# A four-layer graph network on one core: layer 0 multiplied in bfloat16 and float16 parts, and attention's scores in batches of three and five

## The chip, the core and the metric

The kernel runs on one core of a Trainium2 chip, as one program. The metric is the device time of one execution in microseconds (us). The engines that matter are TensorE (PE; its weight loads are listed apart as PEld), VectorE (DVE), ScalarE (ACT), GpSimd (POOL) and SyncE (SP), whose queue issues nearly all DMAs. The engines run side by side, each through its own instructions in their order; semaphores make one wait for another.

## What is computed

There are 3327 nodes with 128 features each (x, float32), and one adjacency matrix adj, 3327 x 3327, float32, whose entries are 0 or 1 (0.48% are 1). Four layers follow one another; each takes h = relu(layernorm(x)) and adds its result to x:

```python
# layer 0                       # layer 1: attention over all nodes; 128 heads (d) of width 8 (h)
x1 = swish((adj @ h) @ W + b)   q, k, v = (x @ W.T).reshape(d, n, 8)  for Wq, Wk, Wv
x2 = swish((adj @ x1) @ W + b)  a = softmax(q @ k.T * d**-0.5 + adj + adj)
                                out = (a @ v).reshape(n, 8 * d) @ Wo.T
# layer 2: a GRU cell on adj @ h       # layer 3: (S + adj) normalised by degree, times h, where S
                                       # keeps the 4 most similar nodes of each row
```

Layer 1 is by far the largest: 128 heads, each with 3327 x 3327 scores, every one of which goes through an exponential.

## The kernel before

**Tiles.** The nodes are cut into T = 26 tiles of 128; node n sits at partition n // 26, tile n % 26. adj is read through its transpose (`adjT`): one tile is 128 rows of 3327 columns, 1.7 MB.

**Layer 0** (lines 275 to 326). Two products with adj, `adj_matmul` (line 194), one after the other. Each loops over the 26 tiles: load the tile into one of three buffers `a`, then seven matmuls of up to 512 columns in float32 (line 204) into seven PSUM banks. Beside it DVE makes passes over each tile: in the first product the column sums that give the degrees (`colsum`, line 292) and, in every second tile, the maximum over the low 16 bits of the words (`bf16_rest`, line 284), which says whether adj is exact in bfloat16; in the second product the absolute maximum (`a_max`, line 295) and the other half of the low bits. In the second product POOL also makes the doubled bfloat16 copy of the tile's first 476 columns (line 272), which attention uses first. After each product the sum is copied out of PSUM (`evacuate`), multiplied by W in groups of four tiles (line 315) and put through the swish. After the first product 26 small matmuls (`dp`, line 310) turn the column sums into the degrees, and DVE copies them out (line 311). At the end the result x is stored to `x1d` (line 326), for the general path.

**Projections** (lines 422 to 498). For each of the 26 row tiles PE makes q, k and v (1024 columns each), ACT copies them out of PSUM, and SP stores them to DRAM. Between the rows a list `early` is worked off, one entry a row: splitting k and q into two parts (`Parting`), the 20 loads for the first four heads (`load_heads(0, 0)`, 16 for k and q and 4 for v, issued at once), the exponentials of the first mask tiles (`exp_of`), and POOL's copies of the keys (`key_pair`). At the end a chain of small operations (lines 484 to 497) reduces four maxima over all partitions and sets the flag `unsafe`.

**Attention** (lines 505 to 631) is written out by hand in a fixed order on all engines (`manual_schedule`). The outer loop runs over 7 chunks of queries (six of 476, one of 471), then over 32 groups of four heads, then over the 26 key tiles t: 5824 steps. In a step:

- `scores` (line 534): four score matmuls, one a head, on 32 rows of PE each (line 547). They go to four buffers `early` and to the tile `late` (one bank in even steps, two in odd steps). The way of a score is a letter: D, DVE adds the mask out of PSUM (line 552); I, PE adds the mask by a product with an identity (`two_i`; the mask tile is already doubled) into the same bank (line 550); G, POOL multiplies by the exponential of the mask afterwards (line 555). Even steps use DDDI, odd steps DDIG.
- ACT takes the exponential of `late` straight from PSUM, once a step (line 553: 476 elements in even steps, 952 in odd ones), and in odd steps the exponential of the pair's five D scores together (line 557: 2380 elements).
- `weigh` (line 559), four steps later: four products with v (line 564), in float32 as two passes each, into one bank `acc`. At the last tile of a group DVE copies `acc` out (`o4`, line 573), and the next group's first product waits for that.

The order on PE is thus, for every step: four scores, one identity product, the four products with v of the step four before.

**Layers 2 and 3** (`tail`) multiply the bfloat16 copy of adj, stored by then as `adj16`, by two float16 parts of the features (`adj_matmul_parts`, line 216; the matmul is line 230). At the very end a flag decides whether a general path runs (a loop of 0 or 1 turns, line 1001); with these inputs it does not.

Of the kernel before, what the change touches and what calls it, by code (L numbers as in the profile page):

```python
# [21 lines left out]
P = 128  # L22
# [11 lines left out]
ROW_PARTS = ((0, 112, T), (112, P - 1, T), (P - 1, P, T - 1))  # L34
SAFE = 60.0
# [19 lines left out]
def kernel(  # L55
# [40 lines left out]
    nc.vector.memset(xs[96:P, T - 1, :], 0.0)  # L96
    for p0, p1, n in ROW_PARTS:
        nc.sync.dma_start(xs[p0:p1, :n], dram(x_in, p0 * T * D, [[T * D, p1 - p0], [D, n], [1, D]]))
# [34 lines left out]

    CUTS = (0, T // 6, T // 2, T)
# [85 lines left out]
    def adj_matmul_parts(agg, parts, pool, on_tile=None):  # L220

        cs = chunks(N, 512)
        with tc.tile_pool(name="adj_ps", bufs=1, space=PSUM) as ps:
            acc = [ps.tile([P, 512], F32, name=f"agg_ps{c}") for c in range(len(cs))]
            for t in range(T):
                a = pool.tile([P, N], BF16, name="a16")
                nc.sync.dma_start(a, adj16[t])
                for i, part in enumerate(parts):
                    for c, (c0, w) in enumerate(cs):
                        nc.tensor.matmul(  # L230
                            acc[c][:, :w],
                            part[:, t, :],
                            a[:, c0 : c0 + w],
                            start=(t == 0 and i == 0),
                            stop=(t == T - 1 and i == len(parts) - 1),
                        )
                if on_tile is not None:
                    on_tile(t)
            evacuate(agg, acc)
# [19 lines left out]
    x1d = dpool.tile([P, T, D], F32, name="x1d")  # L259
# [14 lines left out]

    with tc.tile_pool(name="l0", bufs=1) as pool:
        h, done = layernorm_relu(pool)
        done(T)
        colsum = pool.tile([P, NP], F32, name="colsum")
        nc.vector.memset(colsum[:, N:NP], 0.0)

        def bf16_rest(t, kp, a):

            words = a.bitcast(U16).rearrange("p (n two) -> p n two", two=2)
            nc.vector.tensor_reduce(low_bits[:kp, t : t + 1], words[:kp, :, 0], AX.X, ALU.max)

        def add_degree(t, kp, a):
            if t % 2 == 0:
                bf16_rest(t, kp, a)
            if t == 0:
                nc.vector.tensor_copy(colsum[:, :N], a)  # L290
            else:
                nc.vector.tensor_add(colsum[:kp, :N], colsum[:kp, :N], a[:kp])

        def abs_max(t, kp, a):
            nc.vector.tensor_reduce(a_max[:kp, t : t + 1], a[:kp], AX.X, ALU.max, apply_absolute_value=True)
            if t % 2:
                bf16_rest(t, kp, a)
            a_first.append(doubled(adj_pools[0], a[:kp, : q_chunks[0][1]], t, q_chunks[0][1]))

        for step, lhs in ((0, h), (1, None)):  # L300
            if step == 1:
                lhs = x1
            agg = new_agg(pool)
            adj_matmul(agg, lhs, add_degree if step == 0 else abs_max)
            x1 = pool.tile([P, T, D], F32, name="x1")
            with tc.tile_pool(name="l0_ps", bufs=3, space=PSUM) as ps:
                if step == 0:
                    dp = ps.tile([P, T], F32, name="dp", bufs=1)
                    for t in range(T):
                        nc.tensor.matmul(dp[:, t : t + 1], slots(colsum)[:, t, :], ones, start=True, stop=True)  # L310
                    nc.vector.tensor_copy(deg, dp)
                for t0, n in quads():
                    mp = ps.tile([P, 4, D], F32, name="mp")
                    for j in range(n):
                        nc.tensor.matmul(mp[:, j, :], slots(agg)[:, t0 + j, :], w0_s, start=True, stop=True)
                    y = x1[:, t0 : t0 + n, :]
                    nc.vector.tensor_add(y, mp[:, :n, :], over_f(b0_s, n))
                    nc.scalar.activation(y, y, AF.Silu)  # L318
                    if step == 1:
                        nc.gpsimd.tensor_add(xs[:, t0 : t0 + n, :], xs[:, t0 : t0 + n, :], y)  # L320
# [5 lines left out]
        nc.gpsimd.dma_start(x1d, xs)  # L326
# [65 lines left out]
    def load_heads(c, g):  # L392
# [7 lines left out]
        for i in range(4):  # L400
# [5 lines left out]
        for i in range(4):  # L406
# [4 lines left out]
            )  # L411
        return k_in, q4, v4, []
# [9 lines left out]
    with tc.tile_pool(name="l1", bufs=1) as pool, tc.tile_pool(name="l1_ps", bufs=3, space=PSUM) as ps:  # L422
# [22 lines left out]
        for g in range(2):  # L445
            part = Parting(g)
            for side in range(2):
                early.append(lambda part=part: (part.load(0), part.load(1)) if part.lo[0] is None else None)
                early.append(lambda part=part, side=side: [part.part(side, i) for i in range(4)] and part.store(side))
        first, e_first = [], []  # L450
        early.append(lambda: first.extend(load_heads(0, 0)))
        ahead_part = Parting(2)
        early.append(lambda: (ahead_part.load(0), ahead_part.load(1)))
        early.append(lambda: e_first.extend(exp_of(a, 0) for a in a_first[1::2]))
        early += [lambda: (key_pair(first), key_pair(first))] * (T // 4)
        if T // 2 % 2:
            early.append(lambda: key_pair(first))
        for r in range(T):
# [13 lines left out]
            s = st.tile([P, NH, EA], F32, name="v_st")  # L472
            nc.gpsimd.memset(s[:, :, E : E + 1], 1.0)
# [7 lines left out]

        mx4 = pool.tile([P, 4], F32, name="mx4")
        for i, m in enumerate((q_max, k_max, a_max, low_bits)):
            nc.vector.tensor_reduce(mx4[:, i : i + 1], m, AX.X, ALU.max)
        all4 = pool.tile([P, 4], F32, name="all4")
        nc.gpsimd.partition_all_reduce(all4, mx4, P, bass_isa.ReduceOp.max)
        bound = pool.tile([P, 1], F32, name="bound")
        nc.vector.tensor_mul(bound, all4[:, 0:1], all4[:, 1:2])  # L490
        nc.vector.tensor_scalar_mul(bound, bound, 1.01 * E / 2)
        nc.vector.tensor_add(bound, bound, all4[:, 2:3])
        fits = pool.tile([P, 2], F32, name="fits")
        nc.vector.tensor_scalar(fits[:, 0:1], bound, SAFE / 2, None, op0=ALU.is_le)
        nc.vector.tensor_scalar(fits[:, 1:2], all4[:, 3:4], 0.0, None, op0=ALU.is_equal)
        nc.vector.tensor_mul(unsafe, fits[:, 0:1], fits[:, 1:2])
        nc.vector.tensor_scalar(unsafe, unsafe, -1.0, 1.0, op0=ALU.mult, op1=ALU.add)
        ctx_st.close()
# [6 lines left out]
    WAYS = ("DDDI", "DDIG")  # L505
    PLACES = ((0, 1, 2, 5), (3, 4, 6, 7))
# [12 lines left out]
    with tc.tile_pool(name="at_in", bufs=1) as a_pool, tc.tile_pool(name="at_p", bufs=3) as p_pool, tc.tile_pool(  # L519
# [16 lines left out]
        def scores(step, heads, a2, e_a, p8):  # L536
# [3 lines left out]
            ways, places = WAYS[t % 2], PLACES[t % 2]  # L540
            n_d = ways.count("D")
            late = ps.tile([P, 4 - n_d, 512], F32, name=f"late{4 - n_d}")
            early = [ps.tile([P, 512], F32, name="early", bufs=4) for _ in range(n_d)]
            for i in (*range(n_d, 4), *range(n_d)):
                r = slice(32 * i, 32 * i + 32)
                sp = early[i] if i < n_d else late[:, i - n_d]
                nc.tensor.matmul(sp[:, :we], pairs[t // 2][r, t % 2, :], q4[r, :we], start=True, stop=ways[i] != "I")  # L547
            for i in range(4):
                if ways[i] == "I":
                    nc.tensor.matmul(late[:, i - n_d, :we], two_i, a2[:, :we], start=False, stop=True)  # L550
            for i in range(n_d):
                nc.vector.tensor_tensor(p8[:, places[i], :we], early[i][:, :we], a2[:, :we], op=ALU.add)  # L552
            nc.scalar.activation(p8[:, places[n_d] : places[3] + 1, :we], late[:, :, :we], AF.Exp)  # L553
            if ways[3] == "G":
                nc.gpsimd.tensor_tensor(p8[:, places[3], :we], p8[:, places[3], :we], e_a[:, :we], op=ALU.mult)  # L555
            if t % 2:
                nc.scalar.activation(p8[:, :5, :we], p8[:, :5, :we], AF.Exp)  # L557
# [20 lines left out]
        with tc.manual_schedule(engines=engines):  # L578
# [7 lines left out]
            for j, step in enumerate(steps):  # L586
# [8 lines left out]
                if t % 2 == 0:  # L595
                    p8 = p_pool.tile([P, 8, QW], F32, name="p8")
                scores(step, heads, a_t[t], e_t[t // 2], p8)
                begun[j] = (step, heads[2], p8)
                if j >= ahead:
                    weigh(*begun.pop(j - ahead))  # L600
# [48 lines left out]
    PART = 4096.0  # L649
# [46 lines left out]
    def tail(general):  # L696


        def adj_product(agg, y, parts, on_tile=None):
            if general:  # L700
                adj_matmul(agg, y, on_tile and (lambda t, kp, a: on_tile(t)), a_pool)
            else:
                adj_matmul_parts(agg, parts, a_pool, on_tile)
# [6 lines left out]
        with ExitStack() as s:  # L710
# [42 lines left out]
            with tc.tile_pool(name="l2_tp", bufs=1, space=PSUM) as tps:  # L753
# [9 lines left out]
                adj_product(agg, h, parts, transpose_quad)  # L763
# [53 lines left out]
            with tc.tile_pool(name="l3_hw", bufs=1, space=PSUM) as tps:  # L817
# [18 lines left out]
                adj_product(agg, y, parts, project_quad)  # L836
                while right:
                    project_quad(1)
            nc.gpsimd.tensor_add(xs, xs, over_f(b2_s, T))
# [161 lines left out]
    with tc.For_i(0, n_once, 1):  # L1001
        with tc.tile_pool(name="ga", bufs=1) as pool:
# [63 lines left out]
        nc.sync.dma_start(xs, x1d)  # L1066
# [43 lines left out]
```

## Time and profile before

| | us |
|---|---|
| three runs: median (lowest to highest) | 11189.97 (11184.46 to 11197.54) |
| the profiled execution, its own time | 11195.14 |
| its span, first to last instruction | 11193.4 |
| PE, ACT, DVE, POOL busy | 10850.5, 10199.3, 9343.1, 6016.3 |
| first matmul of layer 0; of its second product | 26.2; 199.4 |
| first matmul of the projections | 381.2 |
| first addition of attention on DVE; last copy of `acc` | 576.2; 10475.2 |

The profile is one execution. Its page gives the busy time of each engine, the share of 40 slices, the chain that ended last, and the costliest groups of instructions; a group's line shows the source line, the engine, what is written from what, the shape, the count, then the busy time in us, the mean of one in ns, and the idle time ahead of it with what ended it. The trace behind it also gives the busy times of any stretch, the instructions in order of time, and who waited for whom. An instruction's duration reaches from its start to its result; instructions overlap on one engine, so what one costs its engine is the distance from its start to the next start. The granted TensorE clock was 0.989 on average, and 1.00 throughout attention.

### The profile page before, as it was taken

What the parts mean: (1) busy time and instruction counts of PE and PEld (TensorE: products, weight loads), DVE (VectorE), ACT (ScalarE), POOL (GpSimd) and SP (SyncE); (2) the same over time, 40 slices, a digit from 0 to 9 for tenths busy, and PEclk for the clock granted to TensorE, in tenths of its full rate; (3) what the DMA queues carried; (4) which work ended last, traced back from release to release, by engine and by line L of the source; (5) the groups of instructions that cost most, each with busy time, mean ns of one, the idle gap of its engine ahead of it and who ended that gap; (6) DMA issues with size and microseconds to landing.
All of it is one profiled execution on the core that took longest, in us unless ns stands there. A gap on an engine that the chain in (4) does not pass through costs nothing. (4 is left out here: it accounts for less than half of the span.)

```text
span 11193.4 us, 209350 instructions
## 1 busy us (share of the span) xinstructions
PE 10850.5 (97%) x79530; PEld 3005.9 (27%) x79530; DVE 9343.1 (83%) x15429; ACT 10199.3 (91%) x9152; POOL 6016.3 (54%) x6964
## 2 busy tenths in 40 slices
PE   9899999999999999999999999999999999999996
PEld 4322222222222222222222222222222222222453
DVE  8588888888888888888888888888888888888656
ACT  0399999999999999999999999999999999999522
POOL 0277777555555555555555555555555555555203
PEclk9899999999999999999999999999999999999998
DMA  7755554333333333333333333333333332333432
GB/s 264 238 129 120 123 127 109 65 64 64 68 64 62 67 66 63 68 65 61 68 66 63 66 66 61 67 66 61 66 66 61 66 63 55 61 58 58 135 113 97
DMA packets 417541, 942.25 MB, mean 84 GB/s; under 512 B 67936, under 2 KB 345937, under 8 KB 380940
## 3 DMA queue, kind: packets, MB, share of 16 engines
q1 hardware_dynamic: 412762, 918.98, 37.4%
q8 instruction: 627, 10.27, 0.4%
q0 software_dynamic: 3760, 9.78, 0.3%
q14 instruction: 392, 3.21, 0.1%
HBM read 788.78 MB, written 139.71 MB: 83 GB/s over the span
## 5 line engine op out<-in xcount | busy, mean ns | idle before, releaser
L552 DVE TENSOR_TENSOR p<-early,a 128x476 f32<-128x476 f32 (+1 forms) x14560 | 8426.4, 646 | 1369.4 <-PE early L547 1297.5
L557 ACT ACTIVATE p<-p 128x2380 f32<-128x2380 f32 (+1 forms) x2912 | 7568.4, 2599 | 0.4
L564 PE MATMUL acc<-p,v 128*9 128x476 f32 (+1 forms) x46592 | 5748.5, 564 | 15.3 <-ACT p L557 1.4
L553 ACT ACTIVATE p<-late 128x476 f32<-128x476 f32 (+1 forms) x5824 | 5315.4, 1175 | 13.8 <-DMA q<-qt 10.2
L555 POOL TENSOR_TENSOR p<-p,e 128x476 f32<-128x476 f32 (+1 forms) x2912 | 3528.1, 1212 | 3204.3 <-ACT p L553 2998.6
L547 PE MATMUL late<-q,k 32*128 32x476 f32 (+1 forms) x8736 | 2798.2, 478 | 99.5 <-ACT p L553 39.7
L547 PE MATMUL early<-q,k 32*128 32x476 f32 (+1 forms) x14560 | 2843.6, 478 | 9.4 <-DVE p L552 9.4
L419 POOL CAST k<-k_in 128x256 fp32r<-128x256 f32 x2912 | 1936.5, 697 | 886.4 <-DMA k_in<-kt 339.4
L547 PEld LDWEIGHTS late<-q,k 32*128 32x128 f32 x8736 | 1065.4, 181 | 4890.4 <-ACT p L553 4186.2
L550 PE MATMUL late<-a,two_i 128*128 128x476 bf16 (+1 forms) x5824 | 2180.8, 374 | 0.0
L547 PEld LDWEIGHTS early<-q,k 32*128 32x128 f32 x14560 | 1113.0, 181 | 9.9 <-DVE p L552 9.9
L564 PEld LDWEIGHTS acc<-p,v 128*9 128x9 f32 x46592 | 695.2, 88 | 1272.6 <-issue 1185.8
L550 PEld LDWEIGHTS <-two_i 128*128 128x128 bf16 x5824 | 556.2, 96 | 1329.0 <-issue 1329.0
L189 ACT COPY agg<-agg_ps 128x512 f32<-128x512 f32 x15 | 8.2, 591 | 485.5 <-PE agg_ps L204 290.6
L230 PE MATMUL agg_ps<-a,part 128*128 128x512 bf16 (+1 forms) x1092 | 227.0, 369 | 4.3 <-ACT agg L928 3.2
L272 POOL TENSOR_SCALAR a<-a_in 128x476 bf16<-128x476 f32 (+2 forms) x156 | 221.1, 1417 | 0.5
L272 POOL TENSOR_SCALAR a<-a 128x476 bf16<-128x476 f32 (+1 forms) x26 | 36.4, 1400 | 288.1 <-DMA a<-in_adjT_dram 288.1
L923 PE MATMUL sp<-yT,hT 128*128 128x512 f32 (+1 forms) x364 | 170.7, 610 | 12.3 <-ACT agg L928 6.4
L204 PE MATMUL agg_ps<-a,h 128*128 128x512 f32 (+2 forms) x364 | 148.2, 570 | 26.2 <-DVE h L164 26.2
L573 DVE COPY o<-acc 105x476 f32<-105x476 f32 (+1 forms) x224 | 144.5, 645 | 4.6 <-PE acc L564 4.6
L204 PE MATMUL agg_ps<-a,x 128*128 128x512 f32 (+2 forms) x364 | 145.3, 562 | 0.6 <-ACT x L318 0.6
L230 PEld LDWEIGHTS <-part 128*128 128x128 f16 x1092 | 108.6, 99 | 117.7 <-issue 10.3
(236 smaller groups left out, 2592.0 us busy)
## 6 DMA issues: line engine op xcount, KB each, us to landing
k_in<-kt SPq DMA_DIRECT2D x1792, 207.9 KB
v<-vd SPq DMA_DIRECT2D x896, 117.0 KB
a<-in_adjT_dram SPq DMA_DIRECT2D x50, 1663.5 KB
a<-adj SPq DMA_DIRECT2D x78, 831.8 KB
q<-qt SPq DMA_DIRECT2D x1536, 29.8 KB
a_in<-in_adjT_dram SPq DMA_DIRECT2D x125, 238.0 KB
adj<-a SPq DMA_DIRECT2D x156, 119.0 KB
vd<-v_st SPq DMA_DIRECT2D x25, 576.0 KB
```

The lines of the kernel that those rows point to most:

```text
L204: nc.tensor.matmul(acc[c][:, :w], lhs[:kp, t, :], a[:kp, c0 : c0 + w], start=(t == 0), stop=(t == T - 1))
L230: nc.tensor.matmul(acc[c][:, :w], part[:, t, :], a[:, c0 : c0 + w], start=(t == 0 and i == 0), stop=(t == T - 1 and i == len(parts) - 1),)
L272: nc.gpsimd.tensor_scalar(a2[:kp, :w], a, 2.0, None, op0=ALU.mult)
L419: nc.gpsimd.tensor_copy(k, slots(k_in)[:, t : t + 2, :])
L547: nc.tensor.matmul(sp[:, :we], pairs[t // 2][r, t % 2, :], q4[r, :we], start=True, stop=ways[i] != "I")
L550: nc.tensor.matmul(late[:, i - n_d, :we], two_i, a2[:, :we], start=False, stop=True)
L552: nc.vector.tensor_tensor(p8[:, places[i], :we], early[i][:, :we], a2[:, :we], op=ALU.add)
L553: nc.scalar.activation(p8[:, places[n_d] : places[3] + 1, :we], late[:, :, :we], AF.Exp)
L555: nc.gpsimd.tensor_tensor(p8[:, places[3], :we], p8[:, places[3], :we], e_a[:, :we], op=ALU.mult)
L557: nc.scalar.activation(p8[:, :5, :we], p8[:, :5, :we], AF.Exp)
L564: nc.tensor.matmul(acc[32 * i : 32 * i + EA, :w], v4[:kp, i, t, :], p8[:kp, PLACES[t % 2][i], :w], start=(t == 0), stop=(t == T - 1),)
L923: nc.tensor.matmul(sp[:, c0 : c0 + w], slots(zT)[:, t, :], z2T[:, cols], start=True, stop=False)
```

## The change

Four things are changed, all in one diff.

**Layer 0.** Each tile of adj is doubled and copied to bfloat16 by ACT as it comes (`a16`, two buffers), and PE multiplies that copy: in the first product by two float16 parts of h (scaled by 4096), in the second by three bfloat16 parts of x1. DVE's pass over each tile is either the column sum or the low bits; the absolute maxima leave. `colsum` is spread over both products, so `dp` stands after the second one. The float32 version stays as `layer_0_general`, in the general path, together with `projections_general`; the store to `x1d` goes.

**x and the projections.** x is loaded in three pieces. The 20 loads of the first heads go out in pieces between the rows; `v_st` is four fixed tiles whose ones are set once.

**The scores.** A pair of steps is made together: three scores (heads 1, 2, 3 of the even step, all D), then the products with v of an earlier step, then five scores (head 0 of the even step and all heads of the odd one) and two identity products. `late` has three banks and is read by one exponential of 1428 elements.

**The flags.** `a_max` is taken in the products of layers 2 and 3 from the bfloat16 copy, in every second tile of each; the chain that sets `unsafe` moves behind the second of them.

The core of the diff:

```diff
-    for p0, p1, n in ROW_PARTS:
-        nc.sync.dma_start(xs[p0:p1, :n], ...)
+        for t0, t1 in zip(CUTS, CUTS[1:]):
+            for p0, p1, n in ROW_PARTS:
+                ...
+                    nc.sync.dma_start(xs[p0:p1, t0 : t0 + m], ...)
...
+        parts = two_parts(pool)
+        parts3 = [pool.tile([P, T, D], BF16, name=f"part3_{i}") for i in range(3)]
+        with tc.tile_pool(name="adj_in", bufs=3) as a_pool, tc.tile_pool(name="adj_half", bufs=2) as half_pool:
...
+                _, done = layernorm_relu(ln, lambda h, p, n: split(parts, h, p, scale=PART))
...
+                for step, lhs in ((0, parts), (1, parts3)):
...
+                            load_rows(a, adjT, t, 0, N)
+                            a16 = half_pool.tile([P, N], BF16, name="a16")
+                            nc.scalar.activation(a16[:kp], a[:kp], AF.Copy, scale=2.0)
+                            for i, part in enumerate(lhs):
+                                for c, (c0, w) in enumerate(cs):
+                                    nc.tensor.matmul(acc[c][:, :w], part[:kp, t, :], a16[:kp, c0 : c0 + w], ...)
+                            if t % 2 == step:
+                                bf16_rest(t, kp, a)
+                            else:
+                                nc.vector.tensor_add(colsum[:kp, :N], colsum[:kp, :N], a[:kp])
...
+                            if step == 0:
+                                rest = own.tile([P, 4, D], F32, name="x1_rest", bufs=2)
+                                nc.scalar.copy(parts3[0][:, q], y)
+                                nc.vector.tensor_sub(rest[:, :n], y, parts3[0][:, q])
+                                nc.gpsimd.tensor_copy(parts3[1][:, q], rest[:, :n])
+                                nc.vector.tensor_sub(parts3[2][:, q], rest[:, :n], parts3[1][:, q])
...
-        early.append(lambda: first.extend(load_heads(0, 0)))
+        pieces, e_first = [], []
+        first = load_heads(0, 0, pieces)
+        early += pieces[:4]
...
-    WAYS = ("DDDI", "DDIG")
-    PLACES = ((0, 1, 2, 5), (3, 4, 6, 7))
+    WAYS = ("IDDD", "DDIG")
+    PLACES = ((5, 0, 1, 2), (3, 4, 6, 7))
+    BATCHES = (((0, 1), (0, 2), (0, 3)), ((0, 0), (1, 2), (1, 3), (1, 1), (1, 0)))
...
+            late = ps.tile([P, 3, 512], F32, name="late")
+            for n, batch in enumerate(BATCHES):
+                if n == 1:
+                    between()
+                for odd, i in batch:
+                    way, place = WAYS[odd][i], PLACES[odd][i]
+                    sp = ps.tile([P, 512], F32, name="early", bufs=4) if way == "D" else late[:, place - 5]
+                    r = slice(32 * i, 32 * i + 32)
+                    nc.tensor.matmul(sp[:, :we], pairs[t // 2][r, odd, :], q4[r, :we], start=True, stop=way != "I")
+                    if way == "D":
+                        nc.vector.tensor_tensor(p8[:, place, :we], sp[:, :we], a2s[odd][:, :we], op=ALU.add)
+            for odd, i in BATCHES[1]:
+                if WAYS[odd][i] == "I":
+                    nc.tensor.matmul(late[:, PLACES[odd][i] - 5, :we], two_i, a2s[odd][:, :we], start=False, stop=True)
+            nc.scalar.activation(p8[:, 5:, :we], late[:, :, :we], AF.Exp)
+            nc.scalar.activation(p8[:, :5, :we], p8[:, :5, :we], AF.Exp)
...
                 if t % 2 == 0:
-                    p8 = p_pool.tile([P, 8, QW], F32, name="p8")
-                scores(step, heads, a_t[t], e_t[t // 2], p8)
+                    p8 = scores(step, heads, a_t[t : t + 2], lambda: weigh(*begun.pop(j - ahead)) if j >= ahead else None)
+                else:
+                    times_e(step, p8, e_t[t // 2])
+                    if j >= ahead:
+                        weigh(*begun.pop(j - ahead))
...
+            def seen(t, a):
+                if t % 2 == half:
+                    nc.vector.tensor_reduce(a_max[:, t : t + 1], a, AX.X, ALU.max, apply_absolute_value=True)
...
     with tc.For_i(0, n_once, 1):
+        layer_0_general()
+        projections_general()
```

## The prediction

> **What bounds the kernel now.** I read the busy time by stage first, since one average over five stages says little.
>
> ```profile
> core 0: us, PE busy (x) PEld busy (x) DVE busy (x) ACT busy (x) POOL busy (x), PEclk, DMA share, GB/s
> 20.00:175.00 155.00, 148.25 (x364) 70.14 (x365) 149.20 (x53) 6.84 (x10) 0.00 (x0) 1.00 0.71 260
> 381.00:576.00 195.00, 152.40 (x320) 64.77 (x320) 65.16 (x62) 80.12 (x80) 33.63 (x71) 0.87 0.88 264
> 576.00:10475.00 9899.00, 9784.52 (x75704) 2407.52 (x75704) 8533.33 (x14783) 9893.06 (x8814) 5812.77 (x6734) 1.00 0.36 71
> ```
>
> Layer 0's products with adj (the first is row 1) are bound by PE, with DVE close behind; the projections (row 2) by DMA; and attention, 88% of the span, by ACT: 9893 of 9899 us busy. PE has 9785 there, so it is a near second. Attention is 2912 pairs of key tiles, so a pair takes 9899 / 2912 = 3.399 us. The groups by form give what PE and ACT do in a pair, and the timeline when it starts:
>
> ```profile
> L557 ACT ACTIVATE p<-p 128x2380 f32<-128x2380 f32 x2496 | 6491.5, 2601 | 0.4
> L564 PE MATMUL acc<-p,v 128*9 128x476 f32 x38400 | 4744.6, 565 | 11.9 <-DVE o L573 0.7 <-POOL p L555 0.2
> L547 PE MATMUL early<-q,k 32*128 32x476 f32 x12480 | 2439.1, 478 | 9.4 <-DVE p L552 9.4
> L564 PE MATMUL acc<-p,v 128*9 128x471 f32 x6400 | 783.5, 560 | 3.4 <-ACT p L557 1.4
> L547 PE MATMUL early<-q,k 32*128 32x472 f32 x2080 | 404.5, 476 | 0.0
> ```
>
> ```profile
> 5001.26 2.55 ACT L557 ACTIVATE p<-p 128x2380 f32<-128x2380 f32 x1
> ...
> 5002.76 0.49 PE L547 MATMUL late<-q,k 32*128 32x476 f32 x2
> ...
> 5003.18 0.37 PE L550 MATMUL late<-a,two_i 128*128 128x476 bf16 x1
> 5003.34 1.79 ACT L553 ACTIVATE p<-late 128x476 f32<-128x476 f32 x2
> 5003.48 0.12 PEld L564 LDWEIGHTS acc<-p,v 128*9 128x9 f32 x8 [0.21 <-issue]
> 5003.48 0.99 PE L564 MATMUL acc<-p,v 128*9 128x476 f32 x8
> 5004.39 0.18 PEld L547 LDWEIGHTS late<-q,k 32*128 32x128 f32 x1 [0.80 <-ACT p L553]
> 5004.40 0.48 PE L547 MATMUL late<-q,k 32*128 32x476 f32 x1
> ...
> 5004.63 2.57 ACT L557 ACTIVATE p<-p 128x2380 f32<-128x2380 f32 x1
> ```
>
> ACT's row is read start to start: 2.08 for the long exponential, 1.29 for the two from PSUM, together 3.37; there is no gap in it. PE's row: four scores .42, the identity .30, eight products with v .92, so 1.64 a step and 3.28 a pair. PE waits for ACT by about .1 us in every second step and has no other slack. **Whatever adds .1 us to PE's pair is paid in full.**
>
> **Attention, ACT's side.** L553's two calls a pair become one over 1428 elements. From single starts between 2000 and 9000 us, 476 elements hold ACT .447 and 952 hold it .845: .398 for each 476 and .049 fixed. One call costs 3 x .398 + .049 = 1.243, so ACT's pair falls by .049 to 3.32. If ACT remained the bound, that would be 143 us.
>
> **PE's side.** Per pair the scores now go in batches of four and four; in the change three, then five, with products for v after each. Head 0's 32 rows of PE are in the batch of five twice, so I let its fifth score follow the first instead of running beside it. What does one score stream? Durations grow by 478 - 476 = 2 ns for four columns more, while L564's passes grow by 565 - 560 = 5 ns for five: a score's column costs half of what a column of L564 costs. L564's two passes start .403 apart (.85 ns a column), so 476 score columns stream for .20 us; the rest of the .42 is its own weights (0.18 in the PEld row, which starts with the scores and not ahead of them) and .04 for four at once.
> - Batch of three to L564: not in the trace; between .38 (rows where the last score came alone: .376 from its start to L550) and .42. I take .41.
> - Batch of five: .42 + .20 = .62 if the fifth's weights load while the first streams, up to .42 + .20 + .18 = .80 if not. The nearest row is L564's PEld row above: eight weight loads, the second pass's four in the same columns, are all done within .12 us while the first pass still streams. So I take .62.
> - Two identity products in a row: .30 + .20 = .50 (adj's bfloat16 products at L230 take 2.81 us a tile for 6654 columns, .42 ns each).
> - L564 twice: 1.84.
> Sum .41 + .92 + .62 + .50 + .92 = 3.37, .09 above now and .05 above ACT's new pair. PE becomes the bound.
>
> The Trainium skill ("TensorE: Matmul & The Clock Gate", Part 3, "The mechanism") speaks against this change: a weight load overlaps matmuls in flight only where the row group differs, while Part 2 of the page also admits a load into a background buffer. L564's row, all 128 rows in both passes, sides with Part 2; by Part 3's sentence the sum would be 3.55.
>
> **Group ends.** The accumulator is copied out once in 13 pairs (224 times):
>
> ```profile
> 5050.81 0.99 PE L564 MATMUL acc<-p,v 127*9 127x476 f32 x8
> ...
> 5051.91 0.65 DVE L573 COPY o<-acc 105x476 f32<-105x476 f32 x1
> 5052.60 0.12 PEld L564 LDWEIGHTS acc<-p,v 128*9 128x9 f32 x8 [0.35 <-DVE o L573]
> ```
>
> From the last product to the first of the next group at least 1.80 us pass. Today a whole step (1.64) lies between, so .15 is lost, under ACT's cover. In the change only the batch of three does (.92 + .41 = 1.33): .46 is lost, on the engine that bounds. A group takes 13 x 3.37 + .46 = 44.27, 224 of them 9917; minus 10 for the narrower last chunk; plus 31 for the six groups whose 13 mask exponentials (.49 each on ACT) keep ACT the bound (13 x 3.81 = 49.5). 9938 against 9899: **+39 us**. POOL (5813 busy) and DVE (five additions at .56 are 2.8 a pair) stay covered.
>
> **Layer 0.** Now a tile costs PE 5.58 us (float32, starts of consecutive loads) in both products. In bfloat16 two parts cost 2.81, three 4.21. New on ACT: a copy of 3327 elements, 2.8 us by the slope above, beside idle ACT. DVE keeps one pass of 3.61 a tile (the maxima leave). A tile's load is 1.70 MB; at the best rate of the first 60 us (.85 MB in 2 us) it takes 4.0.
> - First product: by the built program's order DVE still meets the mask's identity from POOL (now at 12.6 us) within the first layernorm piece, and its passes over tiles 0 and 2 stand between pieces, so buffers come free late: by my count tile 6 lands near 56 us, then 4.0 to 4.1 a tile; the last is multiplied by 139 (now 174.5).
> - Between the products the 12 us of dp leave, the split into three parts comes. Second product from about 159, PE-bound at 4.21 x 26 = 110, to 268 (now 344.6).
> - dp comes back after it, and DVE's copy of deg waits for it ahead of the layernorm: 2 + 12 + 12 + 22 = 48 to the first projection, now 36.5. So 316 against 381: **-65 us**. Bounds -95 (no load stalls) and -30 (only the first product's gain).
> - Projections: 26 rows, DMA-bound. The 20 loads of the first heads now stand in one block at 471 to 491 us, while PE is 4.3 of 20 us busy; spread over rows they overlap the stores. -15 (0 to -20).
> - Moved work: the 26 maxima (3.61) go to the two bfloat16 products of layers 2 and 3, where DVE is half idle: 0. The small chain with POOL's all-reduce, mask bounds, goes from the start of attention to the path before layer 3's features: +3. The copy of xs to x1d goes, off the path.
>
> **Sum:** +39 - 65 - 15 + 3 = -38 us on the profiled execution's 11195 (span 11193): 11157. The median of the runs shown is 5 lower, inside their spread; I say **11155**.
>
> **Rivals.**
> 1. The fifth score's weights don't hide: +.18 a pair, 13 x 224 x .18 = +524: 11680, slower. For it: nowhere does the trace put the same 32 rows twice in a row. Against: L564's loads. It decides early: beyond .013 us more on PE's pair (38 / 2912) the whole gain is gone.
> 2. PE's pair is cheaper than my sum (.38 for the three, no .04 for crowding) and ACT bounds: a pair of 3.32 to 3.35 gives 30 to 150 us less: about 11040, at the very best 10920. For it: the solo .376 rows. Against: the loss at group ends.
> 3. Layer 0 gives only the first product's 30 us, the projections nothing (DMA at .88 already): 11195 + 39 - 30 = about 11200, no change.
> That the general path runs after all would double the time; adj is 0 and 1, exact in bfloat16, so I give it nothing.
>
> **Chances.** Forecast, 11100 to 11220: .5. Rival 1, whole or in part: .18. Rival 2: .2. Rival 3: .12. Below 11168 (0.2%, about what a measurement of this kernel tells from no change) lie .3 of the first and all of rival 2, so faster .5; same .14 + .07 = .21; slower .29. The range takes rival 2's likely value and a part of rival 1: 11000 to 11300; it leaves out the whole of rival 1.
>
> **What would show it.** PE busiest in attention, ACT idle by some .05 a pair before its call on late; from the batch of five's first score to the first identity product .62 (.80 says rival 1); L564 waiting for o by about .46 a group; first projection near 316 us. If ACT is still busy without gaps, rival 2 holds. I'm wrong if the first projection starts after 350, or the fifth score starts its stream after its own weights.

## The result, and the profile after

| | before | after |
|---|---|---|
| five runs each: median (lowest to highest), us | 11189.82 (11184.46 to 11197.54) | 11244.57 (11243.61 to 11246.85) |
| ratio, 95% interval | | 1.0049 (1.0034 to 1.0064) |
| span of the profiled execution | 11193.4 | 11241.9 |
| first matmul of the projections | 381.2 | 334.8 |
| first addition of attention; last copy of `acc` | 576.2; 10475.2 | 520.7; 10519.2 |

The change made the kernel slower, by half a per cent, where a gain of a third of a per cent was forecast. The stages say where: layer 0 gave 46 us and the projections 9 (195.0 to 185.9), attention took 100 more (9899.0 to 9998.5) and the tail 4.5 (718.2 to 722.7). -46.4 - 9.1 + 99.5 + 4.5 = +48.5, the difference of the spans.

The busy times by stage after the change (first and second product of layer 0, projections, attention):

```profile
core 0: us, PE busy (x) PEld busy (x) DVE busy (x) ACT busy (x) POOL busy (x), PEclk, DMA share, GB/s
20.00:148.00 128.00, 86.59 (x364) 37.87 (x363) 111.65 (x38) 85.48 (x33) 1.45 (x1) 0.93 0.88 344
171.00:288.00 117.00, 113.26 (x546) 54.07 (x545) 90.43 (x30) 73.16 (x28) 30.89 (x25) 0.97 0.80 306
335.00:521.00 186.00, 149.03 (x319) 62.76 (x319) 64.23 (x54) 79.48 (x78) 25.82 (x46) 0.92 0.90 277
521.00:10519.00 9998.00, 9888.54 (x75705) 2446.75 (x75705) 8550.06 (x14783) 9881.84 (x5902) 5814.23 (x6734) 1.00 0.36 70
```

In attention (last row) ACT has 2900 instructions fewer, and the stage is 116 us longer than ACT's busy time; before, the difference was 6. PE's busy time has grown by 104. That does not yet say that PE bounds: the busy times of the two still lie within 7 us of each other. The chain that ended last decides it, here its two lines from the page, shares of the span by engine and by line:

```profile
PE 86%; ACT 5%; DVE 3%; issue 2%; DMA 2%; POOL 1%; SPq 0%; DVEq 0%; ACTq 0%; POOLq 0%
PE acc L661 45%; PE early L641 15%; PE late L646 12%; PE late L641 10%; ACT p L648 2%; ACT p L647 2%; DVE o L670 1%; PE agg_ps L237 1%; DMA a<-in_adjT_dram 1%; POOL rows L1072 0%; ACT e L398 0%; PE yp L840 0%; DMA qf<-qk_st 0%; DVE colsum L325 0%; PE pp L539 0%
```

The end hangs on PE through nearly all of attention. What PE waits for stands in the page's groups, and one pair in the timeline shows PE's order (L641 are scores, L646 identity products, L661 products with v, L647 and L648 ACT's two exponentials):

```profile
L661 PE MATMUL acc<-p,v 128*9 128x476 f32 (+1 forms) x46592 | 5760.7, 564 | 86.4 <-DVE o L670 86.1
L647 ACT ACTIVATE p<-late 128x1428 f32<-128x1428 f32 (+1 forms) x2912 | 3966.0, 1362 | 124.8 <-PE late L646 118.1
```

```profile
5001.87 2.18 ACT L648 ACTIVATE p<-p 128x2380 f32<-128x2380 f32 x1
...
5002.68 0.48 PE L641 MATMUL late<-q,k 32*128 32x476 f32 x3
5002.69 0.28 PEld L641 LDWEIGHTS early<-q,k 32*128 32x128 f32 x2
5002.69 0.69 PE L641 MATMUL early<-q,k 32*128 32x476 f32 x2
...
5003.31 0.57 PE L646 MATMUL late<-a,two_i 128*128 128x476 bf16 x2
...
5003.81 0.99 PE L661 MATMUL acc<-p,v 128*9 128x476 f32 x8
...
5004.00 1.36 ACT L647 ACTIVATE p<-late 128x1428 f32<-128x1428 f32 x1
...
5004.73 0.48 PE L641 MATMUL early<-q,k 32*128 32x476 f32 x3
...
5005.14 0.99 PE L661 MATMUL acc<-p,v 128*9 128x476 f32 x8
5005.26 2.18 ACT L648 ACTIVATE p<-p 128x2380 f32<-128x2380 f32 x1
```

PE's row has no gap; ACT's long call starts 3.39 after the one before. Medians of the distances between 2000 and 9000 us: three scores to L661 .417, that to the batch of five .917, from there to the identity products .628, these to L661 .506, that to the next three .917: 3.385 in all. The last row of the trace that matters is a group's end:

```profile
5037.61 0.99 PE L661 MATMUL acc<-p,v 127*9 127x476 f32 x8
...
5038.53 0.48 PE L641 MATMUL early<-q,k 32*128 32x476 f32 x3
5038.69 0.65 DVE L670 COPY o<-acc 105x476 f32<-105x476 f32 x1
...
5039.40 0.22 PEld L661 LDWEIGHTS acc<-p,v 128*9 128x9 f32 x8 [0.69 <-DVE o L670]
5039.40 1.08 PE L661 MATMUL acc<-p,v 128*9 128x476 f32 x8 [0.39 <-DVE o L670]
...
5040.41 0.48 PE L641 MATMUL late<-q,k 32*128 32x476 f32 x3
```

L661 follows the three scores after .87 and not .417, and the block that then starts is 1.01 long and not .917. The kernel before does not show this second cost, though there, too, the first products of most groups, with their weight loads, wait for the copy (.13 us in the median, behind identity products):

```profile
5052.61 0.99 PE L564 MATMUL acc<-p,v 128*9 128x476 f32 x8
...
5053.52 0.48 PE L547 MATMUL late<-q,k 32*128 32x476 f32 x2
```

That block is .91 long, so the wait alone does not explain the 1.01; why it is longer behind scores was not tried. A group, from one copy of `acc` to the next, takes 44.53 us (median), before 44.04.

### The profile page after: what moved, and what is told of

Its sections match the earlier page's. It is cut to its first block, busy times and chain, and to the rows that moved or that the text cites. A ratio compares the mean times of both kernels' runs of the same rounds, so it can differ in the third digit from the quotient of the medians.

```text
span 11241.9 us, 207120 instructions
## 1 busy us (share of the span) xinstructions
PE 10873.6 (97%) x79712; PEld 2994.8 (27%) x79712; DVE 9379.7 (83%) x15446; ACT 10347.5 (92%) x6301; POOL 6015.1 (54%) x6948
## 4 chain that ended last, share of the span: by engine, by line
PE 86%; ACT 5%; DVE 3%; issue 2%; DMA 2%; POOL 1%; SPq 0%; DVEq 0%; ACTq 0%; POOLq 0%
PE acc L661 45%; PE early L641 15%; PE late L646 12%; PE late L641 10%; ACT p L648 2%; ACT p L647 2%; DVE o L670 1%; PE agg_ps L237 1%; DMA a<-in_adjT_dram 1%; POOL rows L1072 0%; ACT e L398 0%; PE yp L840 0%; DMA qf<-qk_st 0%; DVE colsum L325 0%; PE pp L539 0%
## 5 line engine op out<-in xcount | busy, mean ns | idle before, releaser
L648 ACT ACTIVATE p<-p 128x2380 f32<-128x2380 f32 (+1 forms) x2912 | 6348.9, 2180 | 0.0
L661 PE MATMUL acc<-p,v 128*9 128x476 f32 (+1 forms) x46592 | 5760.7, 564 | 86.4 <-DVE o L670 86.1
L647 ACT ACTIVATE p<-late 128x1428 f32<-128x1428 f32 (+1 forms) x2912 | 3966.0, 1362 | 124.8 <-PE late L646 118.1
L641 PE MATMUL early<-q,k 32*128 32x476 f32 (+1 forms) x14560 | 3413.7, 457 | 10.8 <-DVE p L643 9.6
L641 PEld LDWEIGHTS early<-q,k 32*128 32x128 f32 x14560 | 1372.3, 182 | 2333.5 <-DVE p L643 2329.0
L646 PE MATMUL late<-a,two_i 128*128 128x476 bf16 (+1 forms) x5824 | 1674.7, 369 | 0.0
L641 PE MATMUL late<-q,k 32*128 32x476 f32 (+1 forms) x8736 | 1415.7, 479 | 22.7 <-ACT p L647 22.5
L661 PEld LDWEIGHTS acc<-p,v 128*9 128x9 f32 x46592 | 715.1, 88 | 1917.9 <-issue 1762.6
L641 PEld LDWEIGHTS late<-q,k 32*128 32x128 f32 x8736 | 547.3, 181 | 2345.9 <-ACT p L647 2172.3
L646 PEld LDWEIGHTS <-two_i 128*128 128x128 bf16 x5824 | 330.7, 97 | 964.8 <-issue 964.8
L314 PE MATMUL agg_ps<-a,part 128*128 128x512 bf16 (+2 forms) x910 | 199.9, 381 | 73.6 <-ACT a L311 65.1
L311 ACT ACTIVATE a<-a 128x3327 bf16<-128x3327 f32 (+1 forms) x52 | 154.9, 2979 | 78.7 <-DMA a<-in_adjT_dram 56.9
```

What stands on the lines that cost most here:

```text
L314: nc.tensor.matmul(acc[c][:, :w], part[:kp, t, :], a16[:kp, c0 : c0 + w], start=(t == 0 and i == 0), stop=(t == T - 1 and i == len(lhs) - 1),)
L641: nc.tensor.matmul(sp[:, :we], pairs[t // 2][r, odd, :], q4[r, :we], start=True, stop=way != "I")
L646: nc.tensor.matmul(late[:, PLACES[odd][i] - 5, :we], two_i, a2s[odd][:, :we], start=False, stop=True)
L647: nc.scalar.activation(p8[:, 5:, :we], late[:, :, :we], AF.Exp)
L661: nc.tensor.matmul(acc[32 * i : 32 * i + EA, :w], v4[:kp, i, t, :], p8[:kp, PLACES[t % 2][i], :w], start=(t == 0), stop=(t == T - 1),)
```

## The experiments

Theory T, from these rows: attention is bound by PE; the fifth score (.20 a pair) and the bare group end (.455 + .1) cost more than ACT's merged call saves. Its rivals: the loss comes from another part of the change (R2), or from the merged call and its single buffer `late`, for which both engines wait (R1). Differences below are against the kernel before in the same set of runs; on that scale the change itself stands at +55 us.

### The old order of scores in the changed kernel, and the new order alone in the old one

```diff
 # the first, on the kernel after
-    WAYS = ("IDDD", "DDIG")
-    PLACES = ((5, 0, 1, 2), (3, 4, 6, 7))
-    BATCHES = (((0, 1), (0, 2), (0, 3)), ((0, 0), (1, 2), (1, 3), (1, 1), (1, 0)))
+    WAYS = ("DDDI", "DDIG")
+    PLACES = ((0, 1, 2, 5), (3, 4, 6, 7))
...
 # and scores() and the order of the step as in the kernel before; the second is the reverse, on the kernel before
```

> The changed kernel with the attention steps of the kernel before (batches of four and four, one call on late a step, each score with its own key tile). Theory T (the attention's new order of scores costs 100 us because it makes PE the bound; layer 0, x and the projections gain 46 + 9, the tail loses 4.5): attention back at 9899, first projection at 335, 11190 - 51 = 11139 us. Rival R2 (the attention is slower because of something else that the change moved, such as the maxima and the chain behind them, the first heads' loads or the buffers' places): attention stays near 9998 and the time near 11240.

> The kernel before with nothing but the new order of scores and the merged call on late. T: attention 9998 instead of 9899, all else as before: 11190 + 100 = 11290 us. R2: near 11190. If this and the run with the old scores add up to the whole change (+100 - 51 = +49), the parts do not act on each other.

Measured: old order in the new kernel 11143.2 us, ratio 0.9959 (0.9945 to 0.9973), -45 us; attention 9893. New order alone 11294.2 us, ratio 1.0094 (1.0077 to 1.011), +106 us; attention 9998. Both as T says, R2 is out, and the parts add up (-45 + 106 = +61 against +55, within what the runs scatter). So the forecast's "faster" would have come true for everything but the scores.

### Four and four

```diff
-    BATCHES = (((0, 1), (0, 2), (0, 3)), ((0, 0), (1, 2), (1, 3), (1, 1), (1, 0)))
+    BATCHES = (((0, 1), (0, 2), (0, 3), (1, 0)), ((0, 0), (1, 2), (1, 3), (1, 1)))
```

> The changed kernel with head 0's second score moved from the batch of five to the batch of three: four and four, with the merged call on late and its key tiles kept. T: PE's pair loses the .20 of the fifth score, 3.385 - .20 = 3.18, so ACT bounds again at 3.32 a pair; with some of the group's end still open a group takes 43.2 to 43.7 instead of 44.53, so 185 to 300 us less than the changed kernel: 10945 to 11060. Rival R1 (it is the merged call and the one buffer of late that both engines wait for, not the fifth score): no change, near 11240.

Measured: 11165.2 us, ratio 0.998 (0.9971 to 0.999), -23 us, so 77 less than the change, not the 185 to 300 of T nor R1's nothing. From a batch of four to the identity products it is .422 (median): the fifth score had cost .628 - .422 = .206. But the group only falls to 44.14. The timeline of that run, first PE (a batch with `late`, then one without), then DVE (its additions), then ACT (L648 is the long call):

```profile
5014.84 0.48 PE L641 MATMUL late<-q,k 32*128 32x476 f32 x3
5014.85 0.48 PE L641 MATMUL early<-q,k 32*128 32x476 f32 x1
5015.26 0.57 PE L646 MATMUL late<-a,two_i 128*128 128x476 bf16 x2
5015.76 0.99 PE L661 MATMUL acc<-p,v 128*9 128x476 f32 x8
5016.68 0.86 PE L641 MATMUL early<-q,k 32*128 32x476 f32 x4
5017.47 0.99 PE L661 MATMUL acc<-p,v 128*9 128x476 f32 x8
```

```profile
5014.11 2.90 DVE L643 TENSOR_TENSOR p<-early,a 128x476 f32<-128x476 f32 x5 [0.67 <-PE early L641]
```

```profile
5010.61 2.19 ACT L648 ACTIVATE p<-p 128x2380 f32<-128x2380 f32 x1
...
5014.03 2.18 ACT L648 ACTIVATE p<-p 128x2380 f32<-128x2380 f32 x1
...
5017.35 2.19 ACT L648 ACTIVATE p<-p 128x2380 f32<-128x2380 f32 x1
```

At 5016.68 four scores last .86: three start together and the fourth .38 later, at 5017.06; the last addition of the pair before had ended at 5014.11 + 2.90 = 5017.01. Between 2000 and 9000 us the fourth score comes late in 961 of 2055 pairs, and each time it starts .055 to .057 us after an addition has ended. ACT's calls are 3.42 and 3.32 apart by turns. Part of the expected gain went into a new wait, and the last run on the scores, below, settles which.

### The group's end: hide it, or take its wait away

```diff
 # the first: the new group's first products with v go behind the batch of five
-                    p8 = scores(..., lambda: weigh(*begun.pop(j - ahead)) if j >= ahead else None)
+                    end = j > ahead and t == ahead
+                    p8 = scores(..., lambda: weigh(*begun.pop(j - ahead)) if j >= ahead and not end else None)
+                    if end:
+                        weigh(*begun.pop(j - ahead))
 # the second: the copy does not read the accumulator
-                nc.vector.tensor_copy(o4[: 96 + EA, :w], acc[: 96 + EA, :w])
+                nc.vector.tensor_copy(o4[: 96 + EA, :w], p8[: 96 + EA, 0, :w])
```

> The changed kernel, but once a group, where the first products with v of a new group would follow the last of the old one with only three scores between them, they are put behind the batch of five and the identity products, so that the copy of the accumulator has 1.55 us of PE's work to hide behind and not .42. T: the .455 that PE waits there and the .1 or so in the next block go: .45 to .55 x 223 groups = 100 to 125 us less, 11120 to 11145. Rival: ACT gets its input no sooner because late is late either way, or other work of the group sets its length: less than 40 us.

> The changed kernel, but the copy at the end of a group reads a row block of p8 in SBUF instead of the accumulator, so the first product with v of a new group need not wait for it (left out: the attention's result does not reach the output; all else runs). T: the .455 that PE waits per group and the .1 behind it go, 223 x .45 to .55 = 100 to 125 us less: 11120 to 11145, a group 43.98 to 44.08 instead of 44.53. Rival: ScalarE or another wait takes the place, since ScalarE has only .06 of slack a pair (13 x .06 = .8 a group): less than 60 us.

The second came out as T said: 11124.5 us, ratio 0.994 (0.9923 to 0.9957), so 123 less than the change; a group takes 43.98, .544 less than 44.53, and 223 x .544 = 121. 43.98 / 13 = 3.383 is PE's pair once more.

The first went the other way: 11275.2 us, ratio 1.0076 (1.006 to 1.0093), +87 us, so 33 slower than the change. Its PE at a group's end:

```profile
5009.36 0.99 PE L661 MATMUL acc<-p,v 127*9 127x476 f32 x8
5010.28 0.48 PE L641 MATMUL early<-q,k 32*128 32x476 f32 x3
5010.97 0.49 PE L641 MATMUL late<-q,k 32*128 32x476 f32 x3 [0.20 <-ACT p L647]
5010.98 0.48 PE L641 MATMUL early<-q,k 32*128 32x476 f32 x1
5011.71 0.48 PE L641 MATMUL early<-q,k 32*128 32x476 f32 x1 [0.25 <-DVE p L643]
5012.12 0.57 PE L646 MATMUL late<-a,two_i 128*128 128x476 bf16 x2
5012.63 1.78 PE L661 MATMUL acc<-p,v 128*9 128x476 f32 x16
```

The wait for the copy is gone, but the eight scores now take 1.85 in place of .417 + .628. The batch of five comes .92 earlier, when ACT has not yet emptied `late` (0.20), and its last score needs the bank of the first, whose addition stands on DVE behind the copy of `acc` (0.25). A group grows to 44.65. The step was moved past the queue that frees its buffers, which I had not counted.

### Four and four with the shared bank free

```diff
 # on the kernel with batches of four and four
-                        nc.vector.tensor_tensor(p8[:, place, :we], sp[:, :we], a2s[odd][:, :we], op=ALU.add)
+                        s_in = a2s[odd] if (odd, i) == (1, 1) else sp
+                        nc.vector.tensor_tensor(p8[:, place, :we], s_in[:, :we], a2s[odd][:, :we], op=ALU.add)
```

> The run with batches of four and four came to 11165, where T had said 10945 to 11060: its long exponentials start 3.32 and 3.41 apart by turns, and in every second pair the fourth early score starts .38 after the third. Ring theory: the fifth score that VectorE adds to in a pair shares a bank with the fourth of the next pair, whose product must wait until VectorE's last addition has read it. Here that one addition takes adj's tile twice and does not read the score (left out: one of eight heads' scores), so the bank is free at once; VectorE's work stays. Ring theory: pairs 3.32 throughout and .4 at the group's end, a group 43.55 to 43.65 instead of 44.14, about 115 us less, 11040 to 11055. Rival (VectorE's work itself, or the group's end, sets it): 11150 or more.

Measured: 11067.4 us, ratio 0.9892 (0.9875 to 0.9908), 98 less than four and four (115 expected); the median group is 43.62. ACT in that run:

```profile
5004.65 1.43 ACT L648 ACTIVATE p<-late 128x1428 f32<-128x1428 f32 x1
5005.89 2.26 ACT L649 ACTIVATE p<-p 128x2380 f32<-128x2380 f32 x1
5007.97 1.43 ACT L648 ACTIVATE p<-late 128x1428 f32<-128x1428 f32 x1
5009.21 2.27 ACT L649 ACTIVATE p<-p 128x2380 f32<-128x2380 f32 x1
```

Nearly four of five pairs take 3.31 to 3.34, as here 1.24 + 2.08 = 3.32: the forecast's figure for ACT, to the hundredth. VectorE's additions are not shorter than in the run without the edit (the changed one takes .646 us in the median, the others .644), so it is the bank and not VectorE's work; and the merged call with its one buffer `late` is still there, so R1 is out. So the ring is shown: five additions a pair go through four banks; with a batch of four early scores all four banks must be empty at once, that is after DVE's last addition of the pair before, and DVE starts its additions only when the scores are there. A batch of three leaves a bank over; that is what three and five buys, and the fifth score is its price.

### Layer 0: VectorE's passes, x in pieces, buffers

```diff
 # 1: no pass over the low bits
-                            if t % 2 == step:
-                                bf16_rest(t, kp, a)
-                            else:
+                            if t % 2 != step:
 # 2: x whole
-        for t0, t1 in zip(CUTS, CUTS[1:]): ...
+        for p0, p1, n in ROW_PARTS:
+            nc.sync.dma_start(xs[p0:p1, :n], dram(x_in, p0 * T * D, [[T * D, p1 - p0], [D, n], [1, D]]))
 # 3: with the old scores, three operations of the start on POOL
-                nc.vector.memset(colsum, 0.0)            # and the copy of ident to two_i, and last_row
+                nc.gpsimd.memset(colsum, 0.0)
 # 4: one more buffer for adj's tiles
-        with tc.tile_pool(name="adj_in", bufs=3) as a_pool, ...
+        with tc.tile_pool(name="adj_in", bufs=4) as a_pool, ...
```

> The changed kernel without the pass of VectorE over every second tile that collects adj's low bits (left out: the test whether adj is exact in bfloat16). Theory L (layer 0 gains 46 and not 65 because VectorE, which works off its queue in order, holds the first tiles' buffers until 61 us and puts two tile passes of 3.61 between the third-part splits): the loads reach their pace of 4.2 a tile some 8 us earlier, the first product ends at 140 instead of 148, the second starts 3 to 7 us closer behind it, first projection at 320 to 324 instead of 335, total 11230 to 11234. Rival (the loads alone set the start, and the gap between the products is PE's and ScalarE's): first projection at 332 or later.

> The changed kernel with x loaded whole, as before, instead of in three pieces of columns. In the changed kernel VectorE begins the first layernorm piece at 3.9 us, before it waits for TensorE's identity matrix (from POOL at 10.4); whole, x lands later and that piece's 2.3 us move behind the wait. If the pieces help: first matmul 2 to 4 us later than 24.6, first projection 337 to 340, total 11247 to 11250. If VectorE's queue or the loads of adj hide it: first projection at 335, no change.

> The kernel with the old order of scores (layer 0, x and projections as changed), with three things taken from VectorE's queue at the start and given to POOL: the bfloat16 identity (VectorE waits for it until 10.7), the last-row mask (until 11.7) and the memset of colsum (2.83). Theory L: VectorE is through its first tiles some 6 us earlier, first product ends at 142 instead of 148, total 6 us below the run with the old scores' 11143: 11137. Rival (the loads alone set the start): 11143.

> The changed kernel with four buffers for layer 0's tiles of adj instead of three. Theory B (what the forecast missed in layer 0 is the loads' own: the DMA engines stand idle at 22 to 30, 36 to 38 and 43 to 46 us because no buffer is free, and the last tile of the second product, which loads slowly, is asked for too late): the first product ends some 12 us earlier (136 instead of 148 to 153), the second product's last two tiles no longer wait (111 to 113 us instead of 116 to 117), first projection at 316 to 322, total 11226 to 11232. Rival (VectorE's and ScalarE's passes over the tiles set the pace at the start): first product still takes 124 us from its first matmul, first projection at 332 to 338, no change.

Six profiles with the same layer 0 (the change, old scores, four and four with and without the free bank, both runs on the group's end) put the scale: first matmul at 24.6 to 27.4, first product 123 to 126 long (first to last matmul, mean 124.9), second 113.3 to 117.3 (mean 115.0), first projection at 332 to 338, in the mean 335.3. In the table the stages are those of one profile each; the times of kernels 1 and 2 cannot be told from the change's. Kernel 4 stands at +47 us against the change's +55, and kernel 3 at -50 against -45 for the old scores alone; both intervals overlap with those that they are compared with.

| kernel | first matmul | first product | second product | first projection | time, ratio and interval |
|---|---|---|---|---|---|
| 1 no low bits | 24.8 | 121.2 | 113.7 | 330.8 | 11240.6, 1.0042 (1.0025 to 1.0059) |
| 2 x whole | 31.2 | 126.8 | 113.9 | 342.1 | 11249.4, 1.005 (1.0033 to 1.0067) |
| 3 start on POOL, old scores | 20.6 | 124.0 | 115.7 | 330.2 | 11142.0, 0.9955 (0.9938 to 0.9971) |
| 4 four buffers | 24.8 | 118.8 | 111.3 | 324.8 | 11235.5, 1.0042 (1.0026 to 1.0059) |

Theory L falls for the most part. Without half of VectorE's passes the first product gets 4 us shorter, not 8, and the gap to the second (24 us) stays. The wait that theory L names is there: between 20 and 60 us SP's loads wait 42 us in all for `low_bits` and `colsum`. But without the low bits they wait 23 us for ACT's copies and 13 for `colsum`, so another reader of the buffer takes the place. What VectorE does at the start only shifts the beginning: x whole costs 6 us there (31.2), the three operations 5 (20.6), and the product behind it is as long as ever. The fourth buffer is the one that tells: some 10 us less to the first projection, about 6 of them in the first product and 4 in the second. That is the way theory B said, but less than its 13 to 19 (first projection at 324.8, not at 316 to 322). The transfers between 22 and 46 us, first with three buffers (the change), then with four (GB/s in 40 slices of .6 us):

```profile
GB/s 44 0 0 0 0 0 0 0 0 0 0 0 0 288 67 355 399 399 488 444 355 44 0 0 0 0 288 67 244 421 488 355 444 466 67 0 0 0 0 0
```

```profile
GB/s 421 444 399 444 421 421 311 111 22 22 0 0 0 111 244 288 377 377 399 466 488 89 0 0 0 0 67 266 266 421 377 444 510 377 111 0 0 0 0 0
```

With three buffers none is free from 22 to 29 us. The fourth lets one more load through, to 26; the later holes stay, since every buffer still waits for its passes (SP's loads wait 38 us in all for `low_bits` and `colsum` between 20 and 60 us).

### All that gained, together

Old scores, the start on POOL, four buffers.

> The best version that the runs point to: layer 0, x and projections as changed, the old order of scores, the start's three small operations on POOL, and four buffers for layer 0's tiles. Theory B: first projection at 310 to 318 and 11120 to 11130, against 11143 with the old scores alone. Rival: no further gain, 11137 to 11143.

Measured: 11123.7 us, ratio 0.9943 (0.9926 to 0.9959): 65 us less than before, 120 less than the change and 20 less than the old scores alone (their intervals overlap). First projection at 319.5, a little later than the 310 to 318 expected. It is the fastest kernel here that leaves nothing out.

## Why the prediction was wrong

It had the sign wrong and the mechanism right. The forecast said 11155, the kernel takes 11244.6. That this lies inside the range is luck: the upper part was kept for a share of rival 1, which did not come.

- **The step that failed is the sum of PE's pair, .41 + .92 + .62 + .50 + .92 = 3.37, with the group's end of .46 behind it.** PE is the bound, as the step says, and each term is right to within .01; but the terms are .417, .917, .628, .506 and .917, 3.385 in all. The missing .015 stands 2912 times: 44 us. The group's end is .544 and not .46: the wait is .455 as forecast, and the block behind it is .09 longer, a cost for which the forecast had no term: 223 x .08 = 19 us. Together 63 us, against the 61 by which attention missed (+99.5 where +39 was forecast). Rounding is the smaller part of the .015: medians of the kernel before (.422 for four scores, .305 for an identity product, .917 for the products with v) with the forecast's own .41 and .20 make 3.37 again. What was short are the two terms that no row before showed: three scores alone, .41 for .417, and one more score's columns, .20 for .206. I had written that .013 more on PE's pair takes the whole gain, and yet gave the sum a sign.
- **The fifth score's** mechanism is right: .20 forecast, .206 measured, its weights loaded while the first score is under way. Rival 1 does not hold: .628 to the identity products, not .80. The sentence of the Trainium skill ("TensorE: Matmul & The Clock Gate", Part 3, "The mechanism") that lets weight loads overlap matmuls only in other row groups does not fit these rows, where the same 32 rows do: both early weight loads are through after 0.28 us, and the first score's product ends at .48.
- **ACT's pair**, 3.32: right, seen bare in the last run on the scores. Rival 2 (ACT bounds) does not hold for the change: ACT waited 118 us for the identity products. (30 to 150 us less than 11155 ends at 11005; the 10920 of that rival does not come out of its own terms.)
- **Layer 0** gave 46, not 65; this is the smaller miss, 19 us. Tile 6 was copied at 56.4, as forecast (56). From there the loads took 4.2 a tile (4.0 to 4.1 forecast) and the last one 8.1: last matmul at 147.7 and not 139. The gap to the second product is 23.3 and not 20, the second product 117 and not 109; its last two tiles came late, by about 4 us together. The rest, 47 to the first projection, was right (48). One cause was found by a run: a fourth buffer gives 10 us of the two products' 17 back.
- **Projections** -9 (forecast -15), **tail** +4.5 (+3). Their parts were not tried apart. The 4.3 of 20 us that the forecast gave for 471 to 491 us are PE's busy time between 480 and 500; between 471 and 491 it is 8.4.
- **Rival 3** had layer 0 at 30 and the projections at nothing: it is nearer to the result's sign, for a wrong reason.

In the result +100 us in attention stand against -51 elsewhere. Such a sum has no sign until its terms are known to better than their difference, and mine were not: the range said so, the chances leaned too far to one side.

What stays open: why the last tile's loads are slow (below), and the 24 us between the products, in which VectorE meets two tile passes of 3.61 among the splits:

```profile
150.29 3.60 DVE L286 TENSOR_REDUCE low_bits<-a 128x1 f32<-128x3327 uint16 x1
153.82 1.27 DVE L336 SCALAR_TENSOR_TENSOR x<-mp,b_s 128x512 f32<-128x512 f32 x2
...
158.59 3.61 DVE L325 TENSOR_TENSOR colsum<-colsum,a 128x3327 f32<-128x3327 f32 x1
162.12 1.29 DVE L343 TENSOR_TENSOR x_rest<-x,part 128x512 f32<-128x512 f32 x2
```

Leaving the first pass out did not shorten it; leaving out both was not tried.

## What to carry to other kernels

When a loop runs thousands of times, carry its terms to the nanosecond, from medians of many starts, and multiply each one's own error by the count before giving the sum a sign; the terms that no row shows yet have the largest errors. When two engines are within a few per cent of each other, a saving on the one is worth no more than the other's slack; price the slack first. Before a step is moved to hide a wait, list the buffers that it needs and which engine's queue frees them: an instruction moved forward can wait longer for its bank than it waited where it was.

## What the runs showed of the hardware

- The last tile of adj (112 and 15 rows, two transfers) loads at about half the rate. Between 270 and 276 us a packet of 13 KB took .87 to .92 us (medians of 2 us each) and the engines moved some 230 GB/s while all were busy; four us earlier it was .50 us and 419 GB/s. The same shows at 132 to 138 us (242 GB/s). The cause is open.
- Eight products with v that the copy of `acc` holds up behind three scores take 1.014 us to the next scores in place of .916, at every group's end between 2000 and 9000 us (wait .455). In the kernel before, where the copy holds them up behind an identity product, they take .916 (wait .13). What makes the difference is open.
